# Two layers of attention and FFN on one core: the last batch's delta-rule solve split two and two instead of three and one, the third batch's outputs moved beside the last recurrence

## The chip, the cores and the metric

The kernel runs on one core of a Trainium2 chip. The metric is the device time of one execution in microseconds; lower is better. PE is the matrix engine, DVE the vector engine, ACT the scalar engine, POOL the GpSimd engine, SP the engine that issues nearly all transfers.

## The reference, cut to what matters

Four batches of 512 tokens with 512 channels pass two layers. Each layer normalises x, runs an attention branch s and an FFN branch g, and adds s * silu(g) to x. Only the second layer bears on the change. Its attention is a gated delta rule with 6 heads of 64:

```
S = S * exp(g_t)
u = b_t * (v_t - k_t S)
S = S + k_t u
o_t = (q_t * scale) S
o = o * rsqrt(mean(o*o) + eps) * o_norm_w * silu(gate);  out = o @ Wo.T
```

Its FFN multiplies by the signs of two weight matrices (512 to 2048 and back) with a relu between them.

## The kernel before

A batch is four tiles (t = 0 to 3) of 128 tokens. Within a tile the recurrence is a triangular system: its matrix A comes from products of keys, decays and beta, and U is the inverse of the unit triangle. The kernel gets U for a tile in two stages.

**Small blocks on DVE.** `head_products` (L971) makes A for a tile and sends the 32x32 diagonal blocks to DRAM (`A_d`, L990, 8 transfers). `solve_load` (L995) reads the blocks of several tiles back, one block per partition: 24 partitions per tile. `solve_step` (L1008) is one column of the substitution, a multiply (L1015) and an add (L1019), 31 of them one after the other. `solve_store` (L1021) adds a transposed copy and writes both to `UT_d`. `load_UT` (L1029) brings them into one of three buffers U and T (`Uz`, `Tz`, `NZ = 3`) with 7 transfers per tile.

**Large blocks on PE.** `blocks32`, `blocks32b`, `blocks64`, `blocks64b` (L1039 to L1087) join the 32-blocks to 64 and to 128. Each is a few small matmuls and one to three DVE copies, and each needs the one before.

**The recurrence** over tiles (`recurrence`, L1216): `with_state` (L1090, keys and queries times the state S), `new_values` (L1112, U times the rest), `state` (L1122, the new S), `outputs` (L1136). In step t of its loop the blocks of tile t stand beside the state steps of tile t - 1. It also carries the products of the batch ahead (`within`, L1211: decays, A, W), two steps behind: step t has those of tile t - 2, so a recurrence with a batch ahead has six steps.

**Outputs of a batch.** `out_norms` (L1152), and per tile `gated` (L1163: one transfer, three POOL instructions), `project_out` (L1173: two transfers, three transposes, one ACT copy) and `project_out2` (L1187: six matmuls of 512 columns, one DVE and one POOL instruction, the store). For batches 0 and 1 they lie beside the projections of a later batch. Here all three are called "an output" of a tile.

**FFN pieces.** The FFN of the second layer is cut in 128 pieces (`up1` L909 and `down1` L925, eight matmuls each; between them ACT applies the relu and DVE splits the result in two parts, L892 and L894). They are dealt out between the other steps: `add(w, f, ...)` notes a step with a weight, `part(count)` closes a section, and at the end (L1311) `count` pieces are spread over the section in proportion to the weights. A step `lambda: None` with a weight only makes room for pieces. In a pinned part, the first matmul of a piece is kept behind the PE instruction traced just before it; everything else is ordered by the framework's planner, engine by engine, by its own estimates of when an instruction is ready and, among those ready, by the order of the text. Each engine then runs its list in order.

**The order around the change.** The last batch is batch 3. Recurrence of batch 2 (L1287) with the products of batch 3, six steps, 14 pieces. Then outputs of batch 2 and the solve of tiles 0, 1, 2 of batch 3 in one section (L1290 to L1304) with 15 pieces. Then the recurrence of batch 3 (L1305) with the solve of tile 3 inside it, 15 pieces up to its step 3, and its own outputs in steps 3 and 4 and behind it. `gated`, `outputs` and `project_out2` use DVE instead of POOL for the very last tile.

Of the kernel before, what the change touches and what calls it, by code (L numbers as in the profile page):

```python
# [10 lines left out]
F32 = mybir.dt.float32  # L11
# [22 lines left out]
def kernel(ctx: ExitStack, tc: tile.TileContext, i: dict, out: bass.AP):  # L34
    nc = tc.nc

    def new(pool, shape, dtype, tag, **kw):
        return pool.tile(shape, dtype, tag=tag, name=tag, **kw)
# [765 lines left out]
    def add(w, f, *args):  # L804
        steps.append((w, f, args))
# [222 lines left out]

    def load_UT(b, t):  # L1029
        U, T = Uz[(b * TB + t) % NZ], Tz[(b * TB + t) % NZ]  # L1030
        for k in range(4):
            rows = ds(32 * k, 32)
            nc.sync.dma_start(U[rows, :, rows], UT_d[b, t, :, k, 0].rearrange("h r c -> r h c"))
            if k < 3:
                cols = ds(32 * (k % 2), 32)
                nc.sync.dma_start(T[rows, :, cols], UT_d[b, t, :, k, 1].rearrange("h r c -> r h c"))


    def blocks32(b, t):  # L1039
# [50 lines left out]
    def with_state(b, t):  # L1090
        s = st[b]
        if t == 0:
            s["S"] = new(c0, [P, VC, P], F32, "S")
            nc.gpsimd.memset(s["S"], 0.0)
            s["O"] = new(c0, [P, TB, VD], F32, "O")
            s["so"] = new(c0, [P, TB, NH], F32, "so", bufs=2)
            s["R"] = s["vb", 0]
            return
        S = s["S"]
        pks = bank()  # L1100
        for m in range(VC):
            nc.tensor.matmul(pks[:, ts(m, P)], s["yc", VC + m][:, ts(t, P)], S[:, m, :], start=True, stop=True)
        R = s["R"] = new(c0, [P, VD], F32, "R")
        nc.vector.tensor_tensor(v6(R), v6(pks), bc_in(s["beG"][:, t, :], HD), ALU.mult)
        nc.vector.tensor_tensor(R, s["vb", t], R, ALU.subtract)
        pqs = bank()
        for m in range(VC):
            nc.tensor.matmul(pqs[:, ts(m, P)], s["yc", m][:, ts(t, P)], S[:, m, :], start=True, stop=True)
        tq = s["tq"] = new(c0, [P, VD], F32, "tq")
        nc.vector.tensor_tensor(v6(tq), v6(pqs), bc_in(s["ex"][:, 0, t, :], HD), ALU.mult)  # L1110
# [87 lines left out]

    def solve(b, t0=0, nt=TB):
        l = [(solve_load, b, t0, nt)] + [(solve_step, b, j) for j in range(31)] + [(solve_store, b)]  # L1200
        return l + [(load_UT, b, t) for t in range(t0, min(t0 + nt, NZ))]

# [13 lines left out]
    def recurrence(b, ahead=None, between=(), behind=0):  # L1216
# [6 lines left out]
                if between and t >= behind:  # L1223
                    add(0.0, *between.pop(0))

        for t in range(TB + 2 if ahead is not None else TB + 1):
            other = within(ahead, t - 2) if ahead is not None and t >= 2 else []

            def next_other():
                if other:  # L1230
                    for x in other.pop(0):
                        add(*x)

            if t < TB:
                add(1.0, blocks32, b, t)
            next_other()
# [10 lines left out]
            if t < TB:  # L1247
                add(1.0, blocks64, b, t)
            some(4)
            if 0 < t <= TB:  # L1250
                add(1.0, state, b, t - 1)
                add(1.0, outputs, b, t - 1)
                if t - 1 + NZ < TB and ahead is not None:
                    add(0.0, load_UT, b, t - 1 + NZ)
                if t == 2 and ahead is None:
                    some(40)
                    add(0.0, load_UT, b, NZ)
                if ahead is None:
                    if t == 3:
                        part(TAIL[2], True)  # L1260
                    add(0.0, out_norms, b, t - 1)
                    add(0.0, gated, b, t - 1)
                    for n in range(t - 3, t - 2 if t < TB else TB - 1):
                        if n >= 0:
                            add(0.4, project_out, b, n)
                            add(2.6, project_out2, b, n)
            next_other()
            if t < TB:
                add(1.0, blocks64b, b, t)
            some(4)  # L1270
        left = between

    TAIL, left = (14, 15, 15), []
    for t in range(TB):
        for l in within(0, t):
            for x in l:
# [1 line left out]
    for b in range(NB - 1):  # L1278
        add(0.0, load_xn1, b + 1)
        for n in ORDER[:2]:  # L1280
            add(0.0, load_wp, b + 1, n)
        between = solve(b)
        add(*((0.0,) + between.pop(0)))
        projections(b + 1, between, b - 1 if b else None)
        part(20 if b == 0 else 18)
# [24 lines left out]

    n = 0  # L1311
# [56 lines left out]
```

## Time and profile before

| what | value |
|---|---|
| median of 3 runs | 1554.68 us (1553.83 to 1556.56) |
| the profiled execution | 1553.96 us |
| its span, first to last instruction | 1552.2 us |
| PE, DVE, ACT, POOL busy | 94%, 68%, 41%, 23% of the span |
| mean granted PE clock | 0.982 of full |
| recurrence of batch 2 | 1327.6 to about 1401 us |
| outputs of batch 2, solve of tiles 0 to 2 | about 1401 to 1446 us |
| first block step of batch 3 (L1046) | 1454.06 us |
| last FFN matmul (L930) | about 1515 us |

Busy time counts pipelined matmuls by modelled ends, so a PE that reads 100% is not at its peak. What ends a stage is read from the idle time and what released it, and from the chain of waits; a share over the whole span mixes stages with different limits.

### The profile page before, as it was taken

How to read it: one execution, taken by the hardware profiler on the slowest of the kernel's cores; microseconds unless marked ns; L12 is line 12 of the kernel's file. 1: busy time of each engine (PE TensorE's matmuls, PEld its weight loads, DVE VectorE, ACT ScalarE, POOL GpSimd, SP SyncE). 2: the span in 40 equal slices, each digit the busy share in tenths (PEclk: the TensorE clock that was granted, in tenths of full speed). 3: DMA queues.
4: the chain of work that ended last, by engine and by line, in shares of the span. 5: the costliest groups of instructions: out<-in, count | busy, mean ns of one | idle time of the engine just before them, and what ended most of it. 6: DMA issues, size and time to landing. Idle time of an engine off the chain costs nothing.

```text
span 1552.2 us, 22696 instructions
## 1 busy us (share of the span) xinstructions
PE 1456.8 (94%) x8144; PEld 871.3 (56%) x8144; DVE 1062.9 (68%) x1890; ACT 643.5 (41%) x913; POOL 363.3 (23%) x350
## 2 busy tenths in 40 slices
PE   6999988999999999999998899999999999998897
PEld 3465533455335553456334565786578756875674
DVE  6899744676557655666507659568955897479875
ACT  4655655576546654466433323213231323111012
POOL 1012100222003210133002331153214422245022
PEclk9999999999999999999999999999999999999797
DMA  8956655466005741166015343424452436225423
GB/s 290 336 184 218 216 167 182 150 219 214 24 22 188 227 135 26 61 217 215 22 50 162 112 116 91 128 84 135 131 162 61 140 108 168 78 70 160 120 72 105
DMA packets 192535, 215.90 MB, mean 139 GB/s; under 512 B 66504, under 2 KB 129448, under 8 KB 191528
## 3 DMA queue, kind: packets, MB, share of 16 engines
q1 hardware_dynamic: 189672, 213.33, 43.6%
q10 hardware_dynamic: 2752, 1.14, 0.3%
q8 instruction: 64, 1.05, 0.3%
q14 instruction: 47, 0.39, 0.1%
HBM read 155.22 MB, written 54.58 MB: 135 GB/s over the span
## 4 chain that ended last, share of the span: by engine, by line
PE 62%; DVE 22%; DMA 7%; issue 3%; POOL 2%; ACT 2%; SPq 2%; ACTq 0%; DVEq 0%; POOLq 0%
PE y L333 12%; PE mm L315 11%; PE ph L917 5%; PE y L930 5%; PE sc L401 4%; PE pu L710 3%; PE pu L762 3%; DVE UT L1019 3%; DVE sx L1015 3%; DVE nmx L402 2%; PE pu L1193 2%; DVE yc L718 2%; PE pu L1117 2%; PE mm L432 1%; PE pu L1141 1%
## 5 line engine op out<-in xcount | busy, mean ns | idle before, releaser
L402 DVE TENSOR_REDUCE nmx<-sc 128x2 f32<-128x1024 f32 x256 | 312.4, 1220 | 168.6 <-PE st L422 150.4
L424 ACT ACTIVATE pe<-st 128x1024 f16<-128x1024 f32 x256 | 262.3, 1025 | 130.0 <-PE st L422 129.1
L333 PE MATMUL y<-wdn,hT 128*128 128x512 f32 x512 | 253.8, 620 | 3.2 <-DVE g L337 1.9
L315 PE MATMUL mm<-xr,wc 128*128 128x512 f32 x768 | 205.6, 409 | 0.0
L315 PEld LDWEIGHTS mm<-xr,wc 128*128 128x128 f32 x768 | 136.7, 188 | 48.2 <-issue 21.5
L326 POOL TENSOR_TENSOR hT<-hT,th 128x512 f32<-128x512 f32 x64 | 84.0, 1312 | 328.5 <-ACT hT L325 305.2
L333 PEld LDWEIGHTS y<-wdn,hT 128*128 128x128 f32 x512 | 87.5, 190 | 97.9 <-issue 90.2
L710 PE MATMUL pu<-xn1T,wp 128*128 128x512 f32 x288 | 132.2, 603 | 0.0
L917 PE MATMUL ph<-xsh,sg 128*128 128x512 f32 x256 | 116.3, 454 | 0.0
L422 PE MATMUL st<-qm,kT 32*128 32x512 f16 x512 | 101.9, 385 | 11.0 <-ACT pe L424 11.0
L448 POOL TENSOR_TENSOR oT<-os,sm 128x512 f16<-128x512 f32 x32 | 41.2, 1288 | 299.7 <-DMA sm<-rec_d 262.9
L401 PE MATMUL sc<-kT,qT 32*128 32x512 f16 x512 | 103.6, 385 | 7.2 <-DVE nmx L402 6.4
L922 ACT ACTIVATE hT<-ph,upsc 128x512 f32<-128x512 f32 x64 | 43.8, 685 | 157.9 <-PE ph L917 146.1
L917 PE MATMUL ph<-xsl,sg 128*128 128x512 f32 x256 | 105.2, 411 | 1.5 <-DVE xsl L894 1.5
L401 PEld LDWEIGHTS <-qT 32*128 32x128 f16 x512 | 26.3, 91 | 133.9 <-issue 127.2
L930 PE MATMUL y<-sg,hsh 128*128 128x512 f32 x256 | 87.8, 451 | 6.1 <-DVE hsh L892 5.3
L710 PEld LDWEIGHTS pu<-xn1T,wp 128*128 128x128 f32 x288 | 54.5, 194 | 56.0 <-issue 54.3
L930 PE MATMUL y<-sg,hsl 128*128 128x512 f32 x256 | 76.0, 410 | 0.2 <-DVE hsl L894 0.2
L315 PE MATMUL mm<-xr,fo 128*128 128x512 f32 x256 | 74.0, 423 | 0.9 <-DVE fo L246 0.9
L321 ACT ACTIVATE th<-mm,hwg 128x512 f32<-128x512 f32 x64 | 44.0, 688 | 55.4 <-PE mm L315 54.3
L1015 DVE TENSOR_TENSOR sx<-Ab,UT 96x31 f32<-96x31 f32 (+31 forms) x155 | 64.0, 413 | 3.4
L1019 DVE TENSOR_TENSOR UT<-UT,sx 96x31 f32<-96x31 f32 (+31 forms) x155 | 63.1, 407 | 3.5
(285 smaller groups left out, 2388.3 us busy)
## 6 DMA issues: line engine op xcount, KB each, us to landing
wc<-wS SPq DMA_DIRECT2D x96, 512.0 KB
sg<-sgn_d SPq DMA_DIRECT2D x128, 256.0 KB
wS<-fo SPq DMA_DIRECT2D x16, 1024.0 KB
sm<-rec_d SPq DMA_DIRECT2D x128, 64.0 KB
sgn_d<-sn SPq DMA_DIRECT2D x32, 256.0 KB
raw<-in_w_gateT SPq DMA_DIRECT2D x8, 512.0 KB
hT<-in_w_downT SPq DMA_DIRECT2D x16, 256.0 KB
raw<-in_w_upT SPq DMA_DIRECT2D x8, 512.0 KB
```

Source lines behind the costliest of these rows:

```text
L315: nc.tensor.matmul(pgs[m], wcs[b, c, m][:, h, k, :], xrs[b][:, k, :], start=(k + h == 0), stop=(k == KC - 1 and h == 1))
L326: nc.gpsimd.tensor_tensor(hT, hT, ths[b, c], ALU.mult)
L333: nc.tensor.matmul(ys[t], hTs[b, c][:, ts(t, P)], wdn[:, c, :], start=(c == 0), stop=(c == NI - 1))
L401: nc.tensor.matmul(sc[:, j, :], qTs[n][rows, ts(t, P)], kTs[b, g // 4][rows, :], start=True, stop=True)
L402: nc.vector.tensor_reduce(nmxs[n][:, t, 2 * pr : 2 * pr + 2], sc, AX.X, ALU.max, negate=True)
L422: nc.tensor.matmul(st[:, j, :], kTs[b, g // 4][rows, ts(k, P)], qms[n][rows, :], start=True, stop=True)
L424: nc.scalar.activation(pes[u], st, AF.Exp)
L710: nc.tensor.matmul(pp, wps[b, n][:, k, 0:P], xn1Ts[b][:, k, :], start=(k == 0), stop=(k == KC - 1))
L917: ins = nc.tensor.matmul(ph, sgs[b, c, 0][:, ts(k, P)], xss[b][n][:, k, :], start=(k + n == 0), stop=(k == KC - 1 and n == 1))
L930: ins = nc.tensor.matmul(yss[b][t], hss[b, c][n][:, ts(t, P)], sgs[b, c, 1], start=(c + n == 0), stop=(c == NI - 1 and n == 1))
L1015: nc.vector.tensor_tensor(x, Ab[:, j, j + 1 :].unsqueeze(1).to_broadcast([NBL, j + 1, r]), U[:, 0 : j + 1, j : j + 1].to_broadcast([NBL, j ...
L1019: nc.vector.tensor_tensor(U[:, 0 : j + 1, j + 1 :], U[:, 0 : j + 1, j + 1 :], x, ALU.add)
```

## The change

Six edits, all in the second layer:

1. The last batch's solve is split: tiles 0 and 1 in steps 3 and 4 of batch 2's recurrence, tiles 2 and 3 in steps 0 and 1 of the last recurrence. Four items of the solve are put into the text at each of four places per step: 32 items, the load and all 31 steps, fall into batch 2's recurrence; the store and the two U loads are left over for the section behind it.
2. For that, the products of batch 3 come one step behind instead of two (tile t - 1 in step t), so this recurrence has five steps. `scale_heads` moves from the first place of a step to the last, with the W products.
3. The section between the recurrences has no outputs of batch 2 any more, and 12 pieces instead of 15.
4. The outputs of batch 2 are put into the last recurrence, one per step 1 to 4, behind `new_values` and ahead of `state`. Their buffer O for the last batch takes the place of `z1` in another pool, since the O of batch 2 is still in use. Step 2 begins with an empty step of weight 8. The outputs of batch 3 follow: tile 0 in step 3, tiles 1 and 2 in step 4, tile 3 behind it. This part has 18 pieces instead of 15. All 128 pieces are dealt out by the same place as before, behind `outputs` of step 3.
5. `load_UT` issues the three T transfers first (those of rows 0, 2, 1) and then the four U transfers (1, 3, 0, 2), instead of U and T in turn.
6. `solve` lists the U loads of tiles 2 and 3 as well when it starts behind tile 0.

```
     def load_UT(b, t):
         U, T = Uz[(b * TB + t) % NZ], Tz[(b * TB + t) % NZ]
-        for k in range(4):
+        for k in (0, 2, 1):
+            rows, cols = ds(32 * k, 32), ds(32 * (k % 2), 32)
+            nc.sync.dma_start(T[rows, :, cols], UT_d[b, t, :, k, 1].rearrange("h r c -> r h c"))
+        for k in (1, 3, 0, 2):
             rows = ds(32 * k, 32)
             nc.sync.dma_start(U[rows, :, rows], UT_d[b, t, :, k, 0].rearrange("h r c -> r h c"))
-            if k < 3:
-                cols = ds(32 * (k % 2), 32)
-                nc.sync.dma_start(T[rows, :, cols], UT_d[b, t, :, k, 1].rearrange("h r c -> r h c"))
...
-            s["O"] = new(c0, [P, TB, VD], F32, "O")
+            pool, tag = (c0, "O") if b < NB - 1 else (ce, "z1")
+            s["O"] = new(pool, [P, TB, VD], F32, tag)
...
-        return l + [(load_UT, b, t) for t in range(t0, min(t0 + nt, NZ))]
+        return l + [(load_UT, b, t) for t in range(t0, t0 + nt) if t < NZ or t0]
...
-        for t in range(TB + 2 if ahead is not None else TB + 1):
-            other = within(ahead, t - 2) if ahead is not None and t >= 2 else []
+        early = ahead == NB - 1
+        for t in range(TB + 2 if ahead is not None and not early else TB + 1):
+            other = []
+            if early and t >= 1:
+                first, second, right, left_ = within(ahead, t - 1)
+                other = [[first[1]], second, right, [first[0]] + left_]
+            elif ahead is not None and not early and t >= 2:
+                other = within(ahead, t - 2)
...
+            if t == 2 and ahead is None:
+                add(8.0, lambda: None)
             if t < TB:
                 add(1.0, blocks32, b, t)
...
             some(4)
+            if ahead is None and t > 0:
+                add(0.0, gated, b - 1, t - 1)
+                add(0.4, project_out, b - 1, t - 1)
+                add(2.6, project_out2, b - 1, t - 1)
             if 0 < t <= TB:
                 add(1.0, state, b, t - 1)
                 add(1.0, outputs, b, t - 1)
...
-                if t == 2 and ahead is None:
-                    some(40)
-                    add(0.0, load_UT, b, NZ)
+                if t == 1 and ahead is None:
+                    some(80)
                 if ahead is None:
+                    add(0.0, out_norms, b, t - 1)
                     if t == 3:
-                        part(TAIL[2], True)
-                    add(0.0, out_norms, b, t - 1)
-                    add(0.0, gated, b, t - 1)
-                    for n in range(t - 3, t - 2 if t < TB else TB - 1):
-                        if n >= 0:
-                            add(0.4, project_out, b, n)
-                            add(2.6, project_out2, b, n)
+                        part(18, True)
+                    for n in ((), (), (), (0,), (1, 2))[t]:
+                        add(0.0, gated, b, n)
+                        add(0.4, project_out, b, n)
+                        add(2.6, project_out2, b, n)
...
-        recurrence(b, b + 1, solve(b + 1, 0, 3) if b == NB - 2 else (), TB + 1)
-        part(14 if b < NB - 2 else TAIL[0])
+        recurrence(b, b + 1, solve(b + 1, 0, 2) if b == NB - 2 else (), 3)
+        part((14, 14, 14)[b])
...
     add(0.0, out_norms, b - 1)
-    for t in range(TB):
-        add(0.0, gated, b - 1, t)
-        add(0.4, project_out, b - 1, t)
-        for _ in range(3):
-            if between:
-                add(0.0, *between.pop(0))
-        add(2.6, project_out2, b - 1, t)
-    while between:
-        for _ in range(2):
+    for _ in range(10):
+        for _ in range(4):
             if between:
                 add(0.0, *between.pop(0))
         add(4.0, lambda: None)
-    part(TAIL[1], True)
-    recurrence(b, None, solve(b, 3, 1))
-    for t in range(TB - 1, TB):
-        add(0.4, project_out, NB - 1, t)
-        add(2.6, project_out2, NB - 1, t)
+    part(12, True)
+    recurrence(b, None, solve(b, 2, 2))
+    add(0.0, gated, b, TB - 1)
+    add(0.4, project_out, b, TB - 1)
+    add(2.6, project_out2, b, TB - 1)
     part(len(pieces), True)
```

More of the change, by code (lines that the diff above doesn't have):

```diff
@@ L1271, in recurrence @@
         left = between
-    TAIL, left = (14, 15, 15), []
+    left = []
     for t in range(TB):
@@ L1284 @@
         projections(b + 1, between, b - 1 if b else None)
-        part(20 if b == 0 else 18)
-        recurrence(b, b + 1, solve(b + 1, 0, 3) if b == NB - 2 else (), TB + 1)
-        part(14 if b < NB - 2 else TAIL[0])
+        part((20, 18, 18)[b])
+        recurrence(b, b + 1, solve(b + 1, 0, 2) if b == NB - 2 else (), 3)
+        part((14, 14, 14)[b])
     b, between = NB - 1, left
     add(0.0, out_norms, b - 1)
-    for t in range(TB):
-        add(0.0, gated, b - 1, t)
-        add(0.4, project_out, b - 1, t)
-        for _ in range(3):
-            if between:
-                add(0.0, *between.pop(0))
-        add(2.6, project_out2, b - 1, t)
-    while between:
-        for _ in range(2):
+    for _ in range(10):
+        for _ in range(4):
             if between:
```

## The prediction

> **What bounds the kernel now.** I read the page first, for the share of the chain that ended last by engine, and then only the stretch the change touches, 1330 us to the end.
>
> ```profile
> span 1552.2 us, 22696 instructions
> ...
> PE 62%; DVE 22%; DMA 7%; issue 3%; POOL 2%; ACT 2%; SPq 2%; ACTq 0%; DVEq 0%; POOLq 0%
> ```
>
> PE bounds most of the kernel, so the time lies where PE is not full. The table of stretches shows where (us, then the busy time of PE, weight loads, DVE, ACT and POOL, then the granted PE clock):
>
> ```profile
> 1330.00:1369.00 39.00, 39.00 (x433) 31.96 (x432) 23.22 (x48) 5.18 (x9) 13.09 (x14) 1.00 0.24 62
> 1369.00:1404.00 35.00, 32.60 (x260) 24.80 (x258) 27.33 (x48) 9.23 (x16) 16.17 (x16) 1.00 0.31 92
> 1404.00:1446.00 42.00, 34.99 (x119) 23.11 (x120) 39.87 (x78) 5.14 (x9) 17.21 (x15) 0.92 0.49 160
> 1446.00:1453.00 7.00, 6.33 (x28) 4.96 (x27) 4.40 (x10) 1.38 (x2) 1.27 (x2) 1.00 0.76 211
> 1453.00:1485.50 32.50, 29.11 (x255) 23.16 (x255) 25.53 (x69) 2.54 (x4) 0.88 (x1) 0.79 0.31 79
> 1485.50:1516.00 30.50, 30.02 (x300) 24.41 (x299) 22.64 (x60) 6.04 (x10) 7.25 (x7) 1.00 0.20 57
> 1516.00:1526.50 10.50, 6.61 (x41) 4.21 (x39) 9.22 (x18) 5.14 (x7) 5.89 (x5) 0.99 0.38 119
> 1526.50:1552.20 25.70, 18.40 (x51) 10.73 (x51) 8.98 (x17) 3.41 (x6) 2.52 (x2) 0.70 0.34 110
> ```
>
> Batch 2's recurrence (first two rows) is PE's. From 1404 to 1446 DVE is busy 39.87 of 42 us: the solve of tiles 0 to 2 is the bound there. In the last two rows PE is neither full nor fast: that is the dependent tail. The timeline of PE shows what it costs:
>
> ```profile
> 1522.30 0.94 PE L1108 MATMUL pu<-S,yc 128*128 128x128 f32 x6
> 1526.58 2.79 PE L1117 MATMUL pu<-R,U 128*128 128x64 f32 x12 [3.34 <-issue]
> 1529.94 2.82 PE L1141 MATMUL pu<-Xv,W 128*128 128x64 f32 x12 [0.57 <-ACT Xv L1120]
> ...
> 1533.98 5.49 PE L1193 MATMUL pu<-woT,ogT 128*128 128x512 f32 x6 [0.57 <-ACT ogT L1184]
> ```
>
> PE has nothing for 3.34 us while DVE makes R, and then runs at half clock to 1540: the twelve L1117 took 1.45 us at 1492, here 2.79; six L1193 take 2.84 at 1544, here 5.49.
>
> **The sum, term by term,** in the profiled execution (span 1552.2; its time 1553.96 is 1.76 more, and 0.72 below the median).
>
> Start of the last recurrence. It needs the U of tile 0, so it waits for the first solve. That one now starts at step 3 of batch 2's recurrence, near 1369: A of tile 1 comes one step earlier than in the trace, where it is made at 1374.7 to 1376.4 and written by 1379. The solve's own DVE time: the multiply with c 1.6 us (1.94 with 72 partitions, 1.21 with 24); 62 instructions that took 31.1 us in the first solve (15.89 + 15.20) and 22.2 in the second (10.98 + 11.21); 62 gaps of 0.03; the copy 1.1. The partitions do not explain the two sums, POOL does: 17.21 us of POOL ran beside the first and 4.34 beside the second. One pair shows it, DVE and then POOL:
>
> ```profile
> 1410.67 1.29 DVE L1015 TENSOR_TENSOR sx<-Ab,UT 72x135 f32<-72x135 f32 x1
> 1412.00 0.30 DVE L1019 TENSOR_TENSOR UT<-UT,sx 72x135 f32<-72x135 f32 x1
> ```
> ```profile
> 1410.54 1.27 POOL L1196 TENSOR_TENSOR x1l<-x1l,g1l 128x512 f32<-128x512 f32 x1 [1.87 <-DVE g1l L1194]
> ```
>
> The same size takes 0.30 alone and 1.29 while POOL runs. From 1369 to 1404 POOL is busy 16.17 us, afterwards with nothing of the section left, so a bit under half of the 8.9 us difference: steps 26. Sum 1.6 + 26 + 1.9 + 1.1 = 30.6. DVE had 35 - 27.33 = 7.67 us free there; I take 0.9 of it, 6.9. So 23.7 is left after 1404, beside four splits of pieces of 0.43 + 0.68: the store goes out at 1404 + 23.7 + 4.4 = 1432, against 1445.39. Bounds: 1427.5 (steps 22.2, all free time used) and 1446 (steps 31.1, none used, all six splits ahead).
>
> From the store to L1046 were 8.7 us (1445.39 to 1454.06), with SP issuing a UT load every 0.48. blocks32 needs T of rows 0 and 2; the second was sixth in the list and is now second, four issues or 1.9 us sooner; 1.5 taken, bounds 0 and 1.9. Start: 1432 + 7.2 = 1439. **Term: -15.** PE has 12 pieces of 1.85 us as cover behind 1404, so it idles some 13 us there.
>
> The Trainium skill's page "GPSIMD Engine Reference", section "1. Specifications", says that GpSimd shares its SBUF interfaces with VectorE and contends with VectorE instructions that have two SBUF inputs; each solve step has two. It gives no price. It speaks against the place of this change, where POOL is busy 16 of 35 us; if every one of them held DVE up, the store would go out some 10 us later and the term would be -5.
>
> Work moved behind that start. Three pieces more, 18 for 15: **+5.6**. Batch 2's four outputs: L1193 11.17 and L1182 2.07 us of PE, **+13.2**. Their DVE part (four L1194, 2.72), the ACT copies (1.90) and POOL's 17 us move too; in the last recurrence POOL was busy 0.88 of 32.5 and 7.25 of 30.5, so it is free for them. Their 16 transfers (gate, x1, g1, out) go into SP's list between the sign loads, which waited there for buffers (twelve over 34 us); I cost that at 0, from -1 (they no longer crowd the U loads) to +4 (the 34 us row's worst wait for signs, 0.7, at four to six places).
>
> What the holes give back. One output (3.3 us) fits the 3.34 us hole at 1523, and then the clock holds: L1117 1.35, L1141 1.4, L1193 2.65 us less. **-8.7**; bounds 0 and -28 (all 15 us of idle PE behind 1453 and 13 lost in two stretches of half clock, 1462 to 1475 and 1526 to 1540).
>
> The Trainium skill's page "TensorE: Matmul & The Clock Gate", section "What's actually happening", says that PE falls to half rate after an idle window of about 3.4 us and is back after one busy window of the same length. The trace differs: at 1462 the clock fell with no gap over 1.5 us in the 6 us before, and both half stretches lasted over 13 us. By the page the fill would be worth 3.3 and about 1.7 us, and the sum would be -1.2.
>
> The second solve. It can start 6.8 us after the store (1445.39 to 1452.19, UT has to land first), 1439, and took 46.6 us with the blocks beside it: 1485.5, and 7.2 to the blocks of tile 2: 1493. PE arrives there at 1439 + 31.4 (1454.1 to 1485.5 in the trace) + 3.3 (an output) + 5.6 (three pieces in the empty step) = 1479. For these 14 us there is work that needs no tile 2: the state steps of tile 1 (5.6), an output (3.3) and four pieces pinned behind those (7.4), together 16.3. **Term 0**, if the planner puts them ahead; 14 if it doesn't. In the trace it did such a thing once: at 1504.68 two L1046 run, the other 22 at 1507.54, behind L1102, L1108 and five piece matmuls.
>
> At nothing: O in the place of z1 (read last by `scale_heads`, before O is written); A, W and kd of batch 3 taking buffers just released in the same step (a wait of one PE instruction, up to 0.5 us in four places, covered by pieces); one iteration less in batch 2's recurrence, with the same work.
>
> Sum: -15 + 5.6 + 13.2 - 8.7 = -4.9, so 1549.1 for this execution, 1549.8 beside the median; I say 1549.5.
>
> **Rivals.**
>
> Slower, one mechanism: the second solve takes the place of the first as the wait. If blocks32 of tile 2 stays ahead in PE's list, PE stands 14 us, the state steps of tile 1 behind it: 1563. It decides once that solve ends more than 16 us behind PE's arrival, or the list is in text order. For it: DVE would be full from 1369 to 1486, and the solve is needed a step sooner than now. Against: the split L1046 above.
>
> It doesn't do what it says: the solve's steps find no room beside batch 2's recurrence, whose DVE has 7.7 us free for 30, and the store goes out at 1443 or later. The start gains 3, not 15: 1561. For it: 16 us of POOL. Against: steps that are ready take any free slot.
>
> Faster: steps at 22.2 and all free time used, store at 1427.5 (-4.5), and half of the half clock at 1462 to 1475 gone because outputs fill the first steps (-3.3): 1541.5. For it: POOL ran beside few DVE instructions there that have both inputs in SBUF.
>
> **How the numbers follow.** Chances: the forecast 0.45 (own range 1544 to 1557: 0.31 faster, 0.12 same, 0.02 slower), faster case 0.20, second solve 0.20, no room 0.15 (0.02 same). Within 0.2% means 1551.6 to 1557.8, about what a measurement of this kernel can tell from no change. That makes faster 0.51, same 0.14, slower 0.35. The range 1538 to 1565 takes in all four; the far ends of the bounds together are what is left out.
>
> **What would show it.** The store L1025 near 1432 and L1046 of the last batch near 1439; PE idle in 1369 to 1439 about 13 us more than now, put down to DVE; the blocks of tile 2 near 1493 with L1102 and L1193 ahead of them; the clock at 1.0 behind the last piece and L1117 there at 1.45. A wait of PE for T or U over 5 us, a store behind 1440, or half clock in the tail again would make it wrong.

## The result, and the profile after

The change made the kernel slower: 1559.91 us median of 8 runs against 1554.02 of before, a ratio of 1.0035 (95% interval 1.0019 to 1.0051). The prediction said 1549.5. The profiled execution of the changed kernel took 1561.5 us with a span of 1559.3. From line 1096 on, a line of the changed kernel has one number more than the same line before; in e9 and e13, below, two more are added ahead of L1046.

From the page of the changed kernel, the span and the shares of the chain that ended last:

```profile
span 1559.3 us, 22704 instructions
...
PE 62%; DVE 22%; DMA 7%; issue 3%; ACT 2%; POOL 1%; SPq 1%; ACTq 0%; DVEq 0%; POOLq 0%
```

The chain has nearly the same shares as before (POOL and SPq one point less); 7 us do not show there. The table of stretches does (us, busy time of PE, weight loads, DVE, ACT and POOL, granted PE clock; the same bounds as before except for the end):

```profile
1369.00:1404.00 35.00, 31.69 (x265) 24.70 (x263) 33.51 (x70) 6.04 (x11) 13.96 (x12) 0.97 0.22 66
1404.00:1446.00 42.00, 36.37 (x222) 26.60 (x222) 34.85 (x87) 6.96 (x10) 9.28 (x9) 0.86 0.48 131
...
1453.00:1485.50 32.50, 25.30 (x123) 18.83 (x121) 24.43 (x60) 3.95 (x7) 6.32 (x5) 0.92 0.39 110
...
1526.50:1559.30 32.80, 21.47 (x70) 12.23 (x68) 15.59 (x27) 6.43 (x10) 9.06 (x8) 0.79 0.44 143
```

DVE is nearly full from 1369 to 1404, 33.51 of 35 us: the first solve is there, as meant. The new hole of PE is in 1453 to 1485.5, 7.2 us idle where it was 3.4. PE's timeline has it in two places:

```profile
1477.10 1.65 PE L930 MATMUL y<-sg,hsh 128*128 128x512 f32 x3 [2.46 <-DVE hsh L892]
...
1484.63 0.28 PE L1046 MATMUL pu<-T,A 32*32 32x32 f32 x2 [4.60 <-DMA T<-UT_d]
1484.84 0.80 PE L1103 MATMUL pu<-S,yc 128*128 128x128 f32 x2
1485.57 0.84 PE L1046 MATMUL pu<-T,A 32*32 32x32 f32 x22
```

The blocks of tile 2 wait 4.60 us for T, and `with_state` of tile 1 (L1103), which needs no tile 2, stands behind them in PE's list. What T waits for is in the chain, start and us of each piece:

```profile
1479.09 3.77 DMA UT_d<-UT
...
1482.87 1.62 DMA T<-UT_d
```

The store of the second solve goes out at 1479.09, takes 3.77 us to land, and the load of T takes 1.62 more. The tail, again PE's timeline:

```profile
1533.04 2.79 PE L1118 MATMUL pu<-R,U 128*128 128x64 f32 x12 [2.65 <-DVE R L1106]
1535.62 0.85 PE L1183 MATMUL pu<-identf,og 128*128 128x128 f32 x3
1537.04 5.26 PE L1194 MATMUL pu<-woT,ogT 128*128 128x512 f32 x6 [0.57 <-ACT ogT L1185]
1542.13 1.45 PE L1142 MATMUL pu<-Xv,W 128*128 128x64 f32 x12
```

The last output of batch 2 (L1183, L1194) does not stand in the hole ahead of `new_values` (L1118) but behind it. The hole is still open, `new_values` is at half clock, and the output runs at half clock too, 5.26 us for 2.84, between `new_values` and `outputs` (L1142) of the last tile.

Cut at three instructions that all these traces have (for the blocks of tile 2 the group of 22 L1046, at 1485.57 here), the span divides like this. The column of the prediction puts its terms where it placed them; e13 and e11 are told below.

| stretch, us | before | predicted | after | cut solve and hole (e13) | faster version (e11) |
|---|---|---|---|---|---|
| to the first L1046 of the last batch | 1454.1 | 1439.1 | 1437.3 | 1438.4 | 1438.7 |
| to the blocks of tile 2 | 31.4 | 40.3 | 48.3 | 33.9 | 46.1 |
| to `outputs` of tile 2 | 29.8 | 36.4 | 34.3 | 36.2 | 26.0 |
| to the end | 36.9 | 31.5 | 39.4 | 32.3 | 31.4 |
| span | 1552.2 | 1547.3 | 1559.3 | 1540.8 | 1542.2 |

Against the sum, the start is 1.8 us better, steps 2 and 3 are 2.1 better, steps 0 and 1 are 8.0 worse and the tail is 7.9 worse. Two terms of the sum are to be explained: the second solve at nothing, and the holes at -8.7.

### The profile page after: what moved, and what is told of

It is laid out like the page before. It is cut to its first block, busy times and chain, and to the rows that moved or that the text cites. A ratio compares the mean times of both kernels' runs of the same rounds, so it can differ in the third digit from the quotient of the medians.

```text
span 1559.3 us, 22704 instructions
## 1 busy us (share of the span) xinstructions
PE 1462.5 (94%) x8144; PEld 873.5 (56%) x8144; DVE 1056.2 (68%) x1890; ACT 643.5 (41%) x913; POOL 363.2 (23%) x350
## 4 chain that ended last, share of the span: by engine, by line
PE 62%; DVE 22%; DMA 7%; issue 3%; ACT 2%; POOL 1%; SPq 1%; ACTq 0%; DVEq 0%; POOLq 0%
PE y L333 14%; PE mm L315 12%; PE ph L917 4%; PE y L930 4%; PE sc L401 4%; DVE sx L1015 3%; DVE UT L1019 3%; PE pu L762 3%; PE pu L710 2%; DVE yc L718 2%; PE pu L1194 2%; DVE nmx L402 2%; PE pu L1118 1%; PE mm L432 1%; PE pu L979 1%
## 5 line engine op out<-in xcount | busy, mean ns | idle before, releaser
L930 PE MATMUL y<-sg,hsh 128*128 128x512 f32 x256 | 87.7, 453 | 6.9 <-DVE hsh L892 3.7
L930 PE MATMUL y<-sg,hsl 128*128 128x512 f32 x256 | 76.6, 411 | 0.0
```

The source lines that it names most:

```text
L930: ins = nc.tensor.matmul(yss[b][t], hss[b, c][n][:, ts(t, P)], sgs[b, c, 1], start=(c + n == 0), stop=(c == NI - 1 and n == 1))
```

## The experiments

Theory W: the second solve has taken the place of the first as the wait, and the output in the tail stands in the wrong place. Its main rival, P: PE's work decides, and idle time only moves from one place to another. Ratios are to the kernel before, whose runs on the same chip had medians of 1551.86 to 1554.27. All edits are to the changed kernel unless the text says otherwise.

| run | what | median us | ratio (95%) |
|---|---|---|---|
| after | the change | 1559.91 | 1.0035 (1.0019 to 1.0051) |
| e1 | the split alone | 1558.09 | 1.0030 (1.0016 to 1.0044) |
| e2 | the outputs alone | 1561.45 | 1.0050 (1.0034 to 1.0065) |
| e3 | last output in the hole | 1558.63 | 1.0018 (1.0002 to 1.0034) |
| e4 | state steps first | 1560.10 | 1.0042 (1.0028 to 1.0057) |
| e5 | second solve cut, loads moved too | 1560.32 | 1.0037 (1.0025 to 1.0049) |
| e6 | more pieces first | 1557.84 | 1.0025 (1.0009 to 1.0041) |
| e7 | two outputs beside the first solve | 1557.85 | 1.0023 (1.0006 to 1.0039) |
| e8 | e3 and e4 | 1553.42 | 1.0003 (0.9988 to 1.0019) |
| e9 | second solve cut in place | 1549.65 | 0.9985 (0.9975 to 0.9996) |
| e10 | e3, e4 and e6 | 1553.35 | 1.0010 (0.9998 to 1.0021) |
| e11 | e3, e4 and e7 | 1545.84 | 0.9964 (0.9952 to 0.9975) |
| e12 | before, an output in its hole | 1551.21 | 0.9993 (0.9984 to 1.0002) |
| e13 | e9 and e3 | 1543.12 | 0.9939 (0.9924 to 0.9954) |
| e14 | e11 and e6 | 1543.80 | 0.9944 (0.9925 to 0.9964) |
| e15 | other buffers at the FFN's end | 1557.63 | 1.0020 (1.0004 to 1.0035) |
| e16 | e15 and e3 | 1552.63 | 0.9992 (0.9975 to 1.0009) |

### Each half alone: e1 and e2

e1 puts the outputs of batch 2 back between the recurrences, with 15 pieces; the products, the solves two and two, and the loads stay as in the change, and the rest of the last recurrence is as before:

```
-            if ahead is None and t > 0:
-                add(0.0, gated, b - 1, t - 1)
-                add(0.4, project_out, b - 1, t - 1)
-                add(2.6, project_out2, b - 1, t - 1)
...
+    for t in range(TB):
+        add(0.0, gated, b - 1, t)
+        add(0.4, project_out, b - 1, t)
+        for _ in range(3):
+            if between:
+                add(0.0, *between.pop(0))
+        add(2.6, project_out2, b - 1, t)
```

> Half of the change: the solve of the last batch split two and two, with the products one step earlier and the new order of the loads; the outputs of batch 2 stay in the section between the recurrences with 15 pieces, and batch 3's outputs where they were before. Theory W (the gain of the early start is lost at step 2 of the last recurrence, where PE stands 7 us and then runs at half clock because the second solve comes late, and a little more in the tail): the store still goes out near 1428 to 1433, but PE is full with outputs and pieces until about 1446, so the last recurrence starts near 1447, seven us earlier than before; the blocks of tile 2 are wanted at 1447 + 31 = 1478 and the second solve is there at about 1485, so some 4 of these 7 us are lost again: 1548 to 1553. Rival S (the split in itself costs: two solves of two tiles take more of DVE than three and one, and the wait moves to the second solve wherever the outputs are): 1556 to 1562, with PE standing 7 us or more ahead of the blocks of tile 2. Rival P (PE work only changes place, the ends are set by PE being full): 1547, which is before minus the 7 us that PE stood between 1404 and 1446.

Measured: 1.0030, in the range of rival S, but not by its mechanism. The first solve's store went out at 1422.8, the earliest of all, and the last recurrence began at 1459.3, the latest of all. Between them PE had its list of outputs and pieces, and stood 5.45 us for the gated values of POOL (L1171) in it. The second solve was done in time; its steps then held up the blocks of tile 0, which waited 3.12 us for X (L1052) on DVE. So the early solve alone gained nothing: PE had as much work ahead of the start as before.

e2 is the other half, made on the kernel before:

```
-    for t in range(TB):
-        add(0.0, gated, b - 1, t)
...
+    part(12, True)
     recurrence(b, None, solve(b, 3, 1))
...
+            if ahead is None and t > 0:
+                add(0.0, gated, b - 1, t - 1)
+                add(0.4, project_out, b - 1, t - 1)
+                add(2.6, project_out2, b - 1, t - 1)
```

> The other half: the outputs of batch 2 beside the last recurrence, with 12 pieces ahead of it and 18 in it, O in the place of z1; the solve stays three and one, the products two steps behind. The middle section is then left with 12 pieces, 22 us of PE work, beside the solve of three tiles. Theory W: the first solve sets the start; with no outputs beside it POOL is quiet, so its 62 instructions take some 22 us in place of 31.1, the store goes out at about 1438 and the last recurrence starts near 1446; behind that lie 18.8 us more PE work than before, no wait at step 2, and the same output in the tail: 1560 to 1566. Rival P (only PE's work counts, and the outputs fill holes of the recurrence): 1552 to 1556. If the steps stay at 31 us although POOL is quiet, what I read as POOL holding up DVE falls, and the time is 1568 or more.

Measured: 1.0050, as theory W had it. PE's timeline of e2 shows why the outputs can't go without the split:

```profile
1441.23 0.28 PE L1046 MATMUL pu<-T,A 32*32 32x32 f32 x2 [12.70 <-DMA T<-UT_d]
```

PE stands 12.70 us for the first solve. That solve has a second lesson. Its store went out at 1434.8 in place of 1445.4. Some 8 of these 11 us are its steps: the same 62 instructions on 72 partitions took 22.90 us with POOL busy beside 2.5 us of them, and 31.12 us before, with POOL beside 14.1. The rest is mainly the four L1194 of the outputs (2.72 us), which no longer stand between the steps. The instruction that took 1.29 us before, in DVE's timeline of e2:

```profile
1409.22 0.30 DVE L1015 TENSOR_TENSOR sx<-Ab,UT 72x135 f32<-72x135 f32 x1
```

### One loss at a time: e3 and e4

```
+            if t == TB and ahead is None:
+                add(0.0, gated, b - 1, t - 1)
+                add(0.4, project_out, b - 1, t - 1)
+                add(2.6, project_out2, b - 1, t - 1)
             if 0 < t <= TB:
                 add(1.5, new_values, b, t - 1)
...
-            if ahead is None and t > 0:
+            if ahead is None and 0 < t < TB:
                 add(0.0, gated, b - 1, t - 1)
```

> The changed kernel with one thing moved: in step 4 the output of tile 3 of batch 2 stands behind with_state and ahead of new_values, in the hole in which PE waits for R, where my prediction had put it. Theory W with its second place, the tail: new_values is not later by more than 1 us, runs at full clock (1.4 in place of 2.79), and outputs of tile 3 of batch 3 starts 4 to 6 us earlier, so 1554 to 1557. Rival D (the end is set by DVE, ACT and the transfers behind the last outputs and by the load of g1 that comes late, so PE's order does not matter): 1559 to 1561. Rival H (the output in the hole is itself late, since its gated values or its loads are not there, and it holds up new_values): 1561 to 1564.

Measured: 1558.63, between the ranges; against the change 1.0018 for 1.0035, with intervals that overlap. PE's timeline of e3 shows half of the effect:

```profile
1533.26 5.01 PE L1194 MATMUL pu<-woT,ogT 128*128 128x512 f32 x6 [0.57 <-ACT ogT L1185]
1538.11 1.45 PE L1118 MATMUL pu<-R,U 128*128 128x64 f32 x12
```

`new_values` runs at full clock now, but the output in the hole runs at half clock, and so is longer than the hole. The tail is 35.5 us, not 39.4.

e4 puts `with_state` and `new_values` of tile 1 ahead of the blocks of tile 2:

```
+            late = t == 2 and ahead is None
-            if t < TB:
+            if t < TB and not late:
                 add(1.0, blocks32, b, t)
...
                 add(1.5, new_values, b, t - 1)
             next_other()
+            if late:
+                add(1.0, blocks32, b, t)
+                add(1.0, blocks32b, b, t)
```

> The changed kernel with one thing moved: in step 2 of the last recurrence with_state and new_values of tile 1 stand ahead of the blocks of tile 2, so that PE has them, and DVE's part of them, while the second solve is still under way. Theory W: PE stands under 3 us ahead of the blocks of tile 2 in place of 7, and the state chain is two steps further: 1553 to 1556. Rival C (the chain of the blocks of tile 2, four steps with DVE between, sets the end of step 2 whatever stands ahead of it): 1558 to 1561. Rival V (with_state's three DVE instructions go ahead of the solve's steps and hold them up): 1561 to 1564.

Measured: 1560.10, no better than the change. The wait for T fell from 4.60 to 2.38 us, but the 2.2 us of the split ahead of it and half clock stayed, and `new_values` of tile 1 took 2.80 us. From the first L1046 to the blocks of tile 2 it took 46.7 us, hardly less than 48.3, with two steps more in it. Rival C had the right time; the chain of the blocks, its reason, is the same in e9, below, where the time falls.

### The price of the second solve: e5 and e9

e5 cuts the list of the second solve: `(solve_step, b, j) for j in range(8 if t0 else 31)`.

> The changed kernel with the second solve cut to 8 of its 31 steps (the other 23 are left out, so the U of tiles 2 and 3 is not the inverse); all else as it is. It prices the wait of step 2. Theory W (the late second solve is what eats the early start): its store goes out 15 to 20 us sooner, PE finds T of tile 2 there, the 4.6 us of idle and the half clock behind it go, and DVE splits the pieces without delay: 1550 to 1555, level with the kernel before or better. Rival P (PE's work decides: four outputs and three pieces moved behind the start cost what they cost, and the early start only moved idle time from one place to another): 1557 to 1560, with the time lost again in later holes.

Measured: 1.0037, at the upper end of rival P's range, but the edit did something more. The short list used up its places in step 0, so the loads of tiles 2 and 3 came ahead of the blocks of tile 0 in the text. Tile 3 shares its buffer with tile 0, and PE's timeline of e5 has a wait that the change has not:

```profile
1460.44 1.51 PE L1085 MATMUL pu<-U,X 64*64 64x64 f32 x12 [9.71 <-DMA U<-UT_d]
```

So e5 says nothing of the second solve. e9 does it over with all places kept:

```
     def solve_step(b, j):
...
+        if s["sol"][0] == 2 and j >= 8:
+            return
         r = 31 - j
```

> The second solve cut to 8 steps once more, now with its store and its loads at the places in the text that they have in the changed kernel (in the first attempt the shortened list drew the loads of tiles 2 and 3 ahead of the blocks of tile 0, which share a buffer with tile 3 and stood 9.71 us for it). 23 of 31 steps are left out, so the U of tiles 2 and 3 is not the inverse. Theory W (the late second solve is the price): no wait over 2 us in step 1 or ahead of the blocks of tile 2, these begin at 1474 to 1478 in place of 1484.6, and the end is 1550 to 1555. Rival P (PE's work behind the start decides): the blocks of tile 2 begin earlier, but with the same end, 1558 or more, because the time is lost in steps 3 and 4.

Measured: 0.9985, against 1.0035 of the change: 7.8 us, and rival P falls. The blocks of tile 2, in PE's timeline of e9, wait for nothing:

```profile
1470.44 0.57 PE L1048 MATMUL pu<-T,A 32*32 32x32 f32 x24
```

The cut takes away the wait and also 19.5 us of DVE work (the steps took 23.88 us in the change, 4.36 here), so 7.8 us is the price of the second solve as a whole, not of the 4.60 us alone.

### More work ahead of the blocks of tile 2: e6 and e7

e6: `add(8.0, lambda: None)` becomes `add(24.0, lambda: None)`.

> The changed kernel with the empty step at the head of step 2 given weight 24 in place of 8: sixteen piece matmuls (two pieces, 3.7 us at full clock) come ahead of the blocks of tile 2 that stood behind them. Theory W: they run in the 7 us in which PE stood, and the clock does not fall there: 1555 to 1557.5. Rival P (steps 2 and 3 then miss the pieces as cover for the DVE part of their blocks, and stand as much longer): 1559 to 1561. Rival D (PE stood behind the split of a piece by DVE, since DVE is full with the solve; more pieces there only wait for DVE, and delay the solve as well): 1561 to 1564.

e7 divides the outputs of batch 2:

```
-            if ahead is None and t > 0:
+            for n in ((), (), (2,), (3,), ())[t] if ahead is None else ():
...
-    for _ in range(10):
+    for j in range(10):
...
+        if j in (5, 8):
+            add(0.0, gated, b - 1, j // 7)
+            add(0.4, project_out, b - 1, j // 7)
+            add(2.6, project_out2, b - 1, j // 7)
```

> The changed kernel with the outputs of batch 2 divided: tiles 0 and 1 beside the first solve as before, tiles 2 and 3 in steps 2 and 3 of the last recurrence; 12 and 18 pieces as in the change. PE stood 4.6 us and lost 5.7 us to half clock between 1404 and the start, so two outputs (6.6 us) fit there in part. Theory W: the start is 1 to 3 us later, the blocks of tile 2 still come at about 1484 with 3.3 us more work done, and no output of batch 2 is left in the tail: 1553 to 1556. Rival C (POOL beside the first solve holds up DVE, so the store of the first solve and with it everything behind goes out 3 to 4 us later): 1557 to 1561. Rival P: 1559 to 1560, the idle time goes to other places.

Measured: 1.0025 and 1.0023, about two us under the change, and their intervals overlap with its own: neither is shown to differ from it. e6 lies between the ranges of theory W and rival P, e7 in that of rival C, but not by its mechanism. In e7 the start is no later (1436.9) with two outputs ahead of it: they fit time that PE lost there in the change, where it stood 2.42 us for a load of signs and ran at half clock (granted clock 0.83 from 1404 to the start, 0.95 in e7). But the blocks of tile 2 come at 1480.9 behind 6.81 us of idle, and the hole in the tail is open again (3.2 us, `new_values` 2.80).

### The moves together: e8, e10, e11, e14

> The two single moves together: state steps of tile 1 ahead of the blocks of tile 2, and the last output of batch 2 in the hole ahead of new_values of tile 3. Each alone gave 1560.1 and 1558.6 in the medians, 1555.9 and 1557.5 in the spans of its profiled execution, against 1559.9 and 1559.3. If the two losses of the change are these two places and they add up (theory W): 1554 to 1557. If they move idle time and half clock about without taking any away (rival P): 1558 to 1560.

Measured: 1.0003, level with before, 6.1 us under e4 and 2.3 under e3; the second difference is not clear of the noise. By the ratio that is in theory W's range, by the median just under it.

> The changed kernel with three moves: the last output of batch 2 in the hole ahead of new_values of tile 3, with_state and new_values of tile 1 ahead of the blocks of tile 2, and sixteen more piece matmuls ahead of these. The first two together gave 1553.4, the third alone 1557.8 against 1559.9. If the wait for the second solve is still there to be filled (2.5 us ahead of the blocks of tile 2, 2.3 us behind a split, 3.9 us of half clock in that step), 1550 to 1553; if the pieces are then missing in steps 2 and 3, 1553 to 1556.

Measured: 1.0010, in the second range. The third move adds nothing to e8: PE still waited 1.66 us for the second solve, now for U in the blocks of tile 2, and 0.94 us at `new_values` of tile 2, which e8 did not.

> The changed kernel with the outputs of batch 2 divided (tiles 0 and 1 beside the first solve, tile 2 in step 2, tile 3 in the hole ahead of new_values of tile 3) and with_state and new_values of tile 1 ahead of the blocks of tile 2. Theory W, that every place where PE stands or runs at half clock should get work that waits for nothing: the 6.8 us of idle ahead of the blocks of tile 2 in the divided kernel are filled in part by the state steps, the tail has its hole filled: 1548 to 1552. Rival P (idle time only moves): 1554 to 1558.

Measured: 0.9964, faster than both kernels, by 5.6 us than before, with nothing left out; the five runs lie under theory W's range, on a chip where before took 1551.86. It has the wait for the second solve still, but smaller:

```profile
1484.75 0.68 PE L1046 MATMUL pu<-T,A 32*32 32x32 f32 x24 [1.85 <-DMA T<-UT_d]
```

The gain is behind it. Two outputs fewer than in the change lie behind its start, one of them behind the blocks of tile 2, and its tail takes 31.4 us, at a clock of 0.99.

> The version with the divided outputs, the state steps first and the last output in the hole (0.9964 of before), with the empty step of step 2 at weight 24 in place of 8. It stood 1.85 us ahead of the blocks of tile 2 and lost 3.4 us to half clock in that stretch. If that wait is still for the second solve and pieces can fill it: 0.994 to 0.996, 1543 to 1546. If the pieces are missing as cover in steps 2 and 3: 0.997 to 1.000.

Measured: 0.9944 (0.9925 to 0.9964), in the first range; the interval overlaps that of e11, so the two are not told apart.

### The two terms by themselves: e12 and e13

e12 is the kernel before with the output of tile 1 of batch 3 moved into its own hole:

```
+            if t == TB and ahead is None:
+                add(0.4, project_out, b, 1)
+                add(2.6, project_out2, b, 1)
             if 0 < t <= TB:
                 add(1.5, new_values, b, t - 1)
```

> The kernel before, with one thing moved: the output of tile 1 of batch 3 stands in step 4 between with_state and new_values of tile 3, in the 3.34 us hole, not behind the outputs of tile 3. It prices the term of my prediction that failed, a hole of the tail filled, without anything else of the change. If the term holds (the output costs nothing in the hole and the clock stays at full): new_values takes 1.4 in place of 2.79 and begins no more than 1 us later, 1547 to 1551. If the output runs into the half clock itself, or the chain of tile 3 behind new_values is not PE's, 1553 to 1556.

Measured: 0.9993, no difference shown. The term held where it was drawn and was lost behind it, as PE's timeline of e12 shows:

```profile
1527.21 1.45 PE L1117 MATMUL pu<-R,U 128*128 128x64 f32 x12
...
1537.96 0.87 PE L1182 MATMUL pu<-identf,og 128*128 128x128 f32 x3 [3.43 <-issue]
1539.45 5.35 PE L1193 MATMUL pu<-woT,ogT 128*128 128x512 f32 x6 [0.62 <-ACT ogT L1184]
```

The hole is filled and `new_values` takes 1.45. But before had three outputs for the tail, and with one of them spent early there is nothing left to cover the last tile's way through DVE and ACT: PE stands 3.43 us there, and the last output runs at half clock. Here the filled hole paid nothing without an output more; the change brings one.

e13 is e9 with the move of e3:

> The changed kernel with the second solve cut to 8 of 31 steps in place (23 are left out, so the U of tiles 2 and 3 is not the inverse) and the last output of batch 2 in the hole ahead of new_values of tile 3. If these two are the whole of what my sum got wrong, the time is what the sum said or better, since they leave its other terms as they were: the cut solve alone gave 0.9985 of before, the hole alone took 1.3 us and beside the state steps 6.7, so 1543 to 1549 (0.994 to 0.998). If the hole is worth only its 1.3 us, or the idle time moves to the end, 1549 to 1551 (0.998 to 0.9995).

Measured: 0.9939, in the first range. Its tail, in PE's timeline:

```profile
1518.78 2.84 PE L1196 MATMUL pu<-woT,ogT 128*128 128x512 f32 x6 [0.57 <-ACT ogT L1187]
1521.46 1.45 PE L1120 MATMUL pu<-R,U 128*128 128x64 f32 x12
1523.48 1.55 PE L1144 MATMUL pu<-Xv,W 128*128 128x64 f32 x12 [0.57 <-ACT Xv L1123]
```

Output, `new_values` and `outputs` follow each other at full clock, and the tail takes 32.3 us, 4.6 less than before although it has an output of 3.3 us more: the hole gives 7.9, where the sum had 8.7. Beside e9, which differs in the place of this output alone, the tail of the profiled execution is 5.8 us shorter (38.1 in e9).

### What holds up the tail ahead of the hole: e15 and e16

With e3 and e8 apart although e4's move alone gained nothing, the tail of the changed kernel was read once more. DVE waits there for a buffer, with U and R of the last tile queued behind; from its timeline:

```profile
1527.47 0.69 DVE L937 TENSOR_TENSOR hT<-y,drow 128x512 f32<-128x512 f32 x1 [2.59 <-DMA g_d<-hT]
```

L937 is the end of the FFN for tile 2. It takes the buffer of tile 0, whose store (g_d) SP had not issued in time. The waits of SP from 1500 to 1530 (us in total, times, longest) say why:

```profile
SPq L1198 <- POOL x1l L1197: 7.6, 2, 5.7
SPq L1178 <- DMA out<-x1l: 3.7, 2, 1.9
```

The store of an output of batch 2 (L1198) stands in SP's list and waits for POOL, and a load waits for that store in turn. Behind them, g_d goes out at 1524.40, 5.5 us after its first DVE step; before it was 3.6. Three kernels without an output of batch 2 in step 3, e11, e12 and e14, have no such wait of DVE. The edit, alone and beside that of e3:

```
-                v = new(d0, [P, DM], F32, "hT")
+                v = new(d0, [P, DM], F32, "hT" if b < NB - 1 or t < 2 else ("hsh", "hsl")[t - 2])
```

> The changed kernel with the end of the FFN of the last batch given other buffers for its tiles 2 and 3 (those of the split, free by then), so that their first DVE step does not wait for the stores of tiles 0 and 1 in SP's list. Theory Q (SP's list, held by the outputs of batch 2, is a third cause of the tail's loss): DVE's wait of 2.59 us and PE's of 1.91 ahead of L1109 go, new_values starts 1.5 to 2.5 us earlier behind outputs of tile 2, 1557 to 1558.5. If it does not matter, since new_values waits for R at half clock anyway: 1559 to 1561.

> The same buffers, and the last output of batch 2 in the hole ahead of new_values. In the profiles the output in the hole took 2.84 us where PE stood 1.26 us or less ahead of L1109 and 4.5 to 5.3 where it stood 1.63 or more. Theory Q: without that wait the clock holds, the output takes 2.84, and the move is worth its 5 to 7 us: 1552 to 1555. If the clock falls there for what came before (the half clock of step 2), the output takes 5 us again: 1557 to 1559.

Measured: 1557.63 and 1552.63, both in the range of theory Q: 2.3 us under the change, and 4.0 under e3, by ratios whose intervals overlap, so neither gain is shown by itself. In both traces L937 waits for nothing and PE's 1.91 us ahead of L1109 are 1.22 and 1.13. The second half of Q's reason does not hold in the profiled execution, though. In the profile of e16 the output in the hole took 5.03 us all the same, behind only 1.13 us of idle PE:

```profile
1532.16 5.03 PE L1194 MATMUL pu<-woT,ogT 128*128 128x512 f32 x6 [0.57 <-DVE so L1162]
```

This execution is the longest of its twelve (1558.54 us; five took 1550.3 or less), and what the others did is not seen. So the wait of DVE is gone, what that is worth is not clear of the noise, and the wait alone does not decide the clock in the hole.

## Why the prediction was wrong, point by point

**The start, -15: right.** The store went out at 1427.9 (1432 said), the first L1046 at 1437.26 (1439 said): -16.8. The steps took 27.2 us (26 said). That POOL beside them is what makes them long is shown by e2. Two misses cancel in part: the store was 4 us sooner than said, and from it to L1046 it took 9.4 us, where 7.2 were said and 8.7 were before. The new order of the loads is not the reason: the second T went out 4.4 us behind the store, 7.1 before. It is PE's own list. The chain that ended last goes there through a load of signs and the pieces behind it, in PE's timeline:

```profile
1432.78 1.62 PE L930 MATMUL y<-sg,hsh 128*128 128x512 f32 x3 [2.42 <-DMA sg<-sgn_d]
```

That load stood in SP's list behind the load of the second solve's blocks (L1000) and the store (L1025), which waited 5.1 and 1.3 us for DVE with the first solve. One reading of the sum was off, too: 17.21 and 4.34 us are POOL's busy time in the stretch; beside the steps themselves it ran 14.1 and 2.7 us.

**The work moved behind it, +5.6 and +13.2: right in size.** In steps 2 and 3 the two outputs made that stretch 4.5 us longer, not 6.6.

**The second solve, 0: wrong, and the first of the two steps that failed.** Its time was right (45.9 us from 1433.2 to the store; 46.6 from 1439 said), and so was PE's arrival (1480; 1479 said). What failed is the cover, 16.3 us of work that needs no tile 2. It was large enough for the 4.60 us that PE stood, but the planner put it behind the blocks of tile 2, not ahead, and where it did start `with_state` early it did so 0.2 us behind the first blocks. The prediction named this as its slower rival, at 14 us and 1563; the price was 7.8 us (e9), since the solve was 6 us earlier than said. The argument for the cover, one split L1046 in the trace of before, was too thin to give it the larger chance. DVE, full with that solve, took its part too: PE stood 2.46 us for the split of a piece. What the order is worth by itself is not shown: e4, with the state steps ahead, was no faster than the change, and the 7.8 us come from leaving out the solve's work together with its wait.

**The holes, -8.7: wrong, the second step that failed.** The size was right (7.9 us in e13) and the place was not: in the text the output is behind `new_values`, the planner kept that order, and the hole stayed. Worse, the output then ran at half clock on the path, 5.26 us. Moved into the hole it gave 2.6 us alone (e3, not clear of the noise), and 6 to 7 beside a mended step 2 (e13 against e9: 0.9939 for 0.9985; e8 against e4: 1.0003 for 1.0042).

**The transfers, 0: some 2.3 us by e15, not clear of the noise; inside the bounds of -1 to +4, but for another reason.** I looked for sign loads behind them. One did come late, ahead of the start, but behind the load of the second solve and the store of the first. What came late behind the transfers of the outputs in SP's list was the first store of the FFN's end, and through a buffer DVE, U and R.

**At nothing: held.** No wait for `scale_heads`, for O or for the buffers of batch 3 shows among those of 0.5 us or more ahead of a PE instruction behind 1404.

**The rival that the solve finds no room** fell with the store at 1427.9.

So the change is not wrong in its idea. It opens 17 us at the start, and needs the order of two steps for what it then has to hide. With the two terms mended the sum holds and more (e13), but e13 leaves out 19.5 us of DVE work, and most of the more, 6.4 us, lies in steps 0 and 1, beside that work (33.9 us for 40.3). Without any work left out the version with divided outputs is 0.9964 of before (e11).

## What to carry to other kernels

When a wait is taken away, ask which instruction stands first in the engine's list when the next one comes, not whether there is work enough to cover it: work that stands behind the waiting instruction covers nothing. Before filling a hole, ask what is left at the place that the work came from (e12), and before moving a transfer into a queue, which buffer that queue frees next (e15). And a shortened list moves its neighbours: keep the places of everything else when you cut one thing (e5 against e9).

## What the runs showed of the hardware

**DVE beside POOL.** The same 62 steps with two inputs took 31.12 us with POOL busy beside 14.1 us of them (before) and 22.90 with 2.5 (e2): 0.7 us lost per us of overlap. With 48 partitions it was 27.2 (11.7; the change, first solve), 28.8 (13.6; e7, first) and 23.1 (3.5; e7, second): 0.5 to 0.6.

**The clock in the tail.** Behind the last `with_state` the first output (six matmuls of 512 columns) took 2.84 us in some profiles and 4.5 to 5.5 in others. Where it stands in the hole, and in the change, the idle time just ahead of L1109 does not tell them apart: 1.63, 1.73 and 1.91 us went with the slow ones (e3, e10, after) and 1.26, 1.00 or none with the fast ones (e8, e13, e11, e12, e14), but e16 was slow behind 1.13 us. In the kernel before, PE stood 2.36 us ahead of 1433; the next four L930 took 1.21 us, full speed, but the granted clock was half from 1434.2 to 1437.6, and the four behind them took 1.74. In all 18 traces the granted clock changes only at the steps of a grid of 3.41 us, which lies differently against the instructions in each: half clock lasted 13.7 us in the tails of before and of the change (four steps), 6.8 in those of e3 and e16, 3.4 in that of e10. Two steps of e16 and two of e8 around L1109 (us, busy time of PE, weight loads, DVE, ACT and POOL, granted PE clock):

```profile
1526.34:1529.76 3.42, 2.29 (x21) 1.77 (x21) 3.35 (x7) 1.80 (x2) 2.35 (x2) 1.00 0.86 298
1529.76:1533.17 3.41, 2.84 (x10) 1.93 (x10) 2.52 (x7) 0.80 (x3) 0.94 (x2) 0.50 0.69 239
```
```profile
1522.16:1525.57 3.41, 2.15 (x22) 1.89 (x22) 2.21 (x6) 1.22 (x2) 1.40 (x2) 1.00 0.63 218
1525.57:1528.98 3.41, 2.59 (x11) 1.41 (x11) 3.12 (x6) 2.01 (x4) 2.48 (x2) 1.00 0.46 154
```

The clock fell behind a step with 2.29 us of PE in it and held behind one with 2.15, so the busy time of one step does not settle it either.

**The same kernel is not always the same.** Executions of e3 lie between 1550.55 and 1561.65 us, with a mean granted clock from 0.975 to 0.984: the five at 0.981 or more took 1550.6 to 1555.3, the seven below it 1558.3 to 1561.7. Nine of e8's twelve took 1551.6 to 1554.4, within the range of e3's five: between these two kernels the share of short executions differs, not what a short one takes. What decides in an execution whether the clock falls at a place is left open. So is why the hole is worth 2.6 us alone and 4 to 7 beside another move (e8, e13, e16): that the moves take half clock from each other fits the traces, but no run shows it.
